# Two row tiles in the last projection of a fused convolution network

## The chip, the core and the metric

The kernel runs on one core of a Trainium2 chip. The metric is device time in microseconds (us) from launch to end, the median of several runs; the profile is one more execution, taken by the hardware profiler. The engines are called as the profile calls them: PE (TensorE, matmuls), PEld (its weight loads), DVE (VectorE), ACT (ScalarE), POOL (GpSimd) and SP (SyncE, which here only issues DMAs). Everything is float32.

## What is computed

The input x holds 8 images of 384 channels by 32 x 32 pixels. Four layers follow each other, each adding to x what it makes of a group normalization of x (32 groups):

```
x = x + conv_attention(gn(x))
x = x + top2_of_4_experts(gn(x))
x = x + depthwise_7x7(gn(x))
x = x + L3(gn(x))
```

The change lies in the last, L3. It makes three branches of the normalized input, mixes them by weights per image and channel, and projects:

```
# branch k of 1, 3, 5: four chunks of 96 channels; chunks 0 and 2 go through
# an MLP (96 -> 12 -> 96, gelu), chunks 1 and 3 through a depthwise k x k conv
a = (x1 + x2 + x3).mean(axis=(2, 3))
g = gelu(a @ fusion_w1 + fusion_b1) @ fusion_w2 + fusion_b2
w = softmax over the 3 branches of g, per image and channel
comb = x1 * w[0] + x2 * w[1] + x3 * w[2]
out = einsum('bchw,cd->bdhw', comb, proj_w) + proj_b
```

## The kernel before

Channels lie on partitions in three tiles of 128 (`NC` = 3), ordered so that the 192 convolved channels come first: all of channel tile 0 (`unit` 0) and the first 64 rows of tile 1. The 64 rows of images q and q + 4 are stacked into one tile of 128 rows, the **pair** q (`unit` 1, four of them; `HB` = 4). An image has `N` = 1024 pixels, worked in two halves of `HF` = 512. The MLPs of all three branches together have 72 hidden rows per image (`MR` = 72); their second matrix is folded with the branch weights and the projection, so that the projection needs only the 72 hidden rows.

**Before the last stage.** The third layer's convolution (`convolve7`, L1065) ends with a group normalization. `fetch3` (L1719 to 1726) loads the four pairs, two DMAs of 64 rows each, eight in all on SP's queue. Four DVE copies (L1849) spread the normalization's scale and shift over the pair's rows (`pair_s`, `pair_t`), ACT applies them (`prepare3`) and DVE transposes the result. The convolutions run as banded matmuls (`convolve3`, L1765 to 1790): unit 1 with 5x5, unit 1 with 3x3, unit 0 with 5x5, unit 0 with 3x3. Between their groups ACT makes banded weights (`wx`, L1539), from `w` which it loads by its own DMA queue, and evicts the sums (`o`, L366). `hidden3` makes the hidden rows and stores them to `hmem`; `reorder` makes copies of the 1x1 branch's input, in the convolutions' row order, in DRAM (`ya0`, `ya1`).

**Branch weights.** During unit 0's 5x5 convolution `branch_mean` and `branch_weights` (L2035 to 2110) run as jobs: PE L2040, a DVE and ACT softmax, and `fac`, the three weights with their scale for each image. POOL's queue then puts `fac` into the convolution's row order by seven DMAs: `fac` to `fmem` in DRAM (L2065, L2067) and from there to `factor` in SBUF (L2072). During the 3x3 convolution of unit 0, `begin` and `complete` (L2120 to 2143) combine the three branches of a unit: a DVE transpose, an ACT scale (L2130), a DVE scalar_tensor_tensor (STT, L2136), then a transpose and an STT more.

**The last stage**, `project3(b)` for b = 0 to 7 (L2180 to L2222). It loads `hid` (72 rows) and `res` (the residual, 3 x 128 rows), completes image b's unit 0 (`c0`), begins that of image b + 1 and, in the first three images, makes the next pair. Six outputs (three channel tiles by two halves) get one PSUM bank each (`po`, six buffers) and three contractions:

- L2197: 72 hidden rows, weights `wm`
- L2200: 128 rows of the pair, with the other image's 64 rows of the weights set to zero
- L2208: 128 rows of `c0`

Between the second and the third PE makes the next image's `wm` in a bank of its own (`pm`, L2149, two buffers), which ACT copies out (L2151). After each L2208 a DVE STT (L2212) adds `po`, the bias `obias` and `res`, and after every second one SP issues the output's DMA (L2219).

The order on PE, DVE, ACT and POOL is the order of the program up to the end of unit 0's 3x3 convolution (`manual_schedule`); in the last stage the build's scheduler sets it, once for all. An engine runs its list in order. A buffer is taken anew when its last reader is done.

Of the kernel before, what the change touches and what calls it, by code (L numbers as in the profile page):

```python
# [18 lines left out]
P = 128  # L19
B, C, H, W = 8, 384, 32, 32  # L20
N = H * W
# [115 lines left out]
def conv_mixer_kernel(ctx: ExitStack, tc: tile.TileContext, a: dict, out: bass.AP):  # L137
# [176 lines left out]
    def affine(o, i, s, t, func=AF.Identity):  # L314
        nc.scalar.activation(o, i, func, bias=t, scale=s)  # L315
# [230 lines left out]
    x2mem = [dram.tile([NC, P, 32 * HP], FP, tag=f"x2_{b}", name=f"x2_{b}") for b in range(B)]  # L546
    y2mem = [dram.tile([NC, P, N], FP, tag=f"y2_{b}", name=f"y2_{b}") for b in range(B)]
    ya0 = [dram.tile([P, N], FP, tag=f"ya0_{b}", name=f"ya0_{b}") for b in range(B)]
    ya1 = [dram.tile([P, N], FP, tag=f"ya1_{q}", name=f"ya1_{q}") for q in range(HB)]
    hmem = [dram.tile([MR, N], FP, tag=f"h{b}", name=f"h{b}") for b in range(B)]  # L550
    fmem = dram.tile([P, 3, B + HB], FP, tag="fac", name="fmem")
    cfmem = dram.tile([2 * B * E * 4, P], FP, tag="cf", name="cfmem")

    def layers(again, early, xst, pre_pool, pp0, pw):
# [1077 lines left out]
        edges = fe.tile([P, 2, B, 5, 4], FP, name="edges")  # L1632
        pair_s, pair_t = (fe.tile([P, HB], FP, name=f"pair_{k}") for k in "st")
        for3 = {}

        def load3():
            for name in "k1 k3 k5 bias3 mw1 mb1 mw2 mw2t fb1 fb2".split():
                for3[name] = load(fe, name)
            for name in ("projb", "proj", "projc"):
                for3[name] = load(fw, name)  # L1640
            gmat["B"] = fe.tile([P, len(blocks), P], FP, name="gmatB")
            nc.sync.dma_start(out=gmat["B"], in_=gmem)

        b7 = load(fe, "b7")
# [74 lines left out]
        def fetch3(q):  # L1719

            y = new_y()
            for half in range(2):
                nc.sync.dma_start(
                    out=y[64 * half : 64 * half + 64, :], in_=y2mem[HB * half + q][1, 0:64, :]
                )
            return y

        def prepare3(unit, q, y=None):

            if unit == 0:  # L1730
                if q == 0:
                    room3(0)
                y = new_xn2().rearrange("p r w -> p (r w)")[:, :N]
                nc.sync.dma_start(out=y, in_=y2mem[q][0])
                affine(y, y, s01[:, 0, q : q + 1], t01[:, 0, q : q + 1])
            else:
                affine(y, y, pair_s[:, q : q + 1], pair_t[:, q : q + 1])
# [10 lines left out]
        def reorder():  # L1748
            def move(o, i):
                nc.gpsimd.dma_start(out=o.rearrange("d r n -> r d n"), in_=i.rearrange("d r n -> r d n"))  # L1750

            for b in range(B):
                ya, y = ya0[b], y2mem[b][0]
                ya = ya.rearrange("(d b a r) n -> b a d r n", a=2, b=2, d=2)
                y = y.rearrange("(a b d r) n -> b a d r n", a=2, b=2, d=2)
                for i, j in product(range(2), repeat=2):
                    move(ya[i, j], y[i, j])
                half, q = b // HB, b % HB
                ya = ya1[q].rearrange("(d b a r) n -> a b d r n", a=2, b=2, d=2)[half]
                y = y2mem[b][1, 0:64, :].rearrange("(b d r) n -> b d r n", b=2, d=2)  # L1760
                for i in range(2):
                    move(ya[i], y[i])
# [41 lines left out]
        with tc.manual_schedule(engines=ORDERED | {mybir.EngineType.Pool}):  # L1804

            for ct in range(NC):
                o = None
                for c in range(8):
# [37 lines left out]
                    if ct == 2 and c == 6:  # L1846
                        for o2, v in ((pair_s, s01), (pair_t, t01)):
                            for half in range(2):
                                nc.vector.tensor_copy(  # L1849
                                    o2[64 * half : 64 * half + 64, :],  # L1850
                                    v[0:64, 1, half * HB : (half + 1) * HB],
                                )
                        for q in range(HB):
                            prepare3(1, q, ys3[q])
# [31 lines left out]
            nc.vector.tensor_copy(s3, s)  # L1886
            nc.vector.tensor_copy(t3, t)
            prepare3(0, 7)
            for _ in range(5):
# [145 lines left out]
            def branch_weights():  # L2035

                pg = banks().tile([P, NC, 3, B])
                for ct in range(NC):
# [19 lines left out]
                for j in range(2):  # L2058
                    nc.vector.tensor_copy(fac[:, j, 1:], wb[:, j, 1:])
                    for o, v in ((fac[:, j, 0], s3), (con[:, j], t3)):  # L2060
# [3 lines left out]
                        )  # L2064
                nc.gpsimd.dma_start(out=fmem[:, :, :B], in_=fac[:, 0])  # L2065
                for half in range(2):
                    nc.gpsimd.dma_start(  # L2067
                        out=fmem[64 * half : 64 * half + 64, :, B:],
                        in_=fac[0:64, 1, :, half * HB : (half + 1) * HB],
                    )  # L2070
                for i in range(4):
                    nc.gpsimd.dma_start(  # L2072
                        out=factor[32 * i : 32 * i + 32],
                        in_=fmem.rearrange("(a b d r) k n -> d b a r (k n)", a=2, b=2, d=2)[
                            i // 2, i % 2
                        ],
                    )

# [61 lines left out]
            def complete(v, unit, q):  # L2140
                c3 = pre.tile([P, N], FP, tag="c3", name="c3")
                nc.vector.transpose(img(c3), os3[unit, 3][:, q])
                add(v, c3, unit, q, 1)

            def weights3(b, pool):

                pm = pool.tile([MR, C], FP, tag="pm", name="pm")
                for j in range(2):
                    nc.tensor.matmul(pm, lhsT=w2[:, j, b], rhs=proj[:, 1 + j], start=j == 0, stop=j == 1)  # L2149
                wm = pre.tile([MR, C], FP, tag="wm", name="wm", bufs=1)  # L2150
                nc.scalar.copy(wm, pm)  # L2151
                return wm

            pairs, c0s, wms = {}, {}, {}

# [4 lines left out]
            def first():  # L2160
                wms[0] = weights3(0, banks(False))
                c0s[0] = begin(0, 0, pre, 2, nc.gpsimd)

# [12 lines left out]
        with tc.tile_pool(name="py", reuse_waits="tile", bufs=2) as py, tc.tile_pool(  # L2176
# [3 lines left out]
            def project3(b):  # L2180
                half, q = b // HB, b % HB
                hid = py.tile([MR, N], FP, tag="hid", name="hid")
                nc.sync.dma_start(out=hid, in_=hmem[b])
                res = py.tile([P, NC, N], FP, tag="res", name="res")
# [4 lines left out]
                if q + 1 < HB and half == 0:  # L2189
                    pair(q + 1, py, HB - 1)  # L2190
                outs = []
                for oc in range(NC):
                    oc_cols = slice(oc * P, (oc + 1) * P)
                    for h in range(2):
                        cols = slice(h * HF, (h + 1) * HF)
                        po = pp.tile([P, HF], FP, tag="pj", name="po")
                        nc.tensor.matmul(  # L2197
                            po, lhsT=wms[b][:, oc_cols], rhs=hid[:, cols], start=True, stop=False
                        )
                        nc.tensor.matmul(  # L2200
                            po, lhsT=projc[:, 1 + half, oc_cols], rhs=pairs[q][:, cols],
                            start=False, stop=False,
                        )
                        outs.append((oc, cols, po))
                if b + 1 < B:
                    wms[b + 1] = weights3(b + 1, pmp)
                for oc, cols, po in outs:
# [3 lines left out]
                    )  # L2211
                    nc.vector.scalar_tensor_tensor(  # L2212
                        out=res[:, oc, cols], in0=po, scalar=obias[:, oc, b : b + 1],
                        in1=res[:, oc, cols], op0=ALU.add, op1=ALU.add,
                    )
                    if cols.start:
# [26 lines left out]
def lay_out(inp):  # L2243
# [78 lines left out]
    for n in KS:  # L2322
        band = np.zeros((2, P, n, W, W), np.float32)
        w = f[f"L3_conv_f{n // 2 + 1}_conv_w"].reshape(192, n, n)
        w = np.concatenate([w, w[P:]]).reshape(2, P, n, n)
# [34 lines left out]

    pc = f["L3_conv_proj_w"][ORDER_B][: 2 * P, ORDER_B].reshape(2, 2, 2, 2, 16, C).swapaxes(1, 3)
    half = np.zeros((2, 2, 2, 2, 16, C), np.float32)
    for h in range(2):
        half[h, :, :, h] = pc[1, :, :, 0]
    o["projc"] = np.concatenate([pc[:1], half]).reshape(3, P, C).swapaxes(0, 1)
    o["projb"] = tiles_b(f["L3_conv_proj_b"])
# [19 lines left out]
```

## Time and profile before

| | us |
|---|---|
| median of 3 runs (3173.9 to 3177.14) | 3174.2 |
| profiled execution | 3172.27 |
| its span, first to last instruction | 3170.5 |
| PE busy | 3023.9 (95% of the span) |
| DVE busy | 1694.7 (53%) |
| ACT busy | 1190.1 (38%) |
| POOL busy | 253.9 (8%) |

In the rows, `L2208 PE MATMUL po<-c,projc 128*128 128x512` means: line 2208, engine PE, a matmul from tiles c and projc into po, with weights of 128 rows by 128 columns and 512 moving columns. A float32 matmul of the program is two PE instructions in the records. `[3.34 <-ACT o L366]` is idle time before the instruction and what ended it. PEclk is the granted TensorE clock as a share of full speed.

The table has the last stage's place in it: PE's first L2197 is at 3030.34 us of the span, its last L2208 ends at 3162.5.

### The profile page before, as it was taken

What the parts mean: (1) busy time and instruction counts of PE and PEld (TensorE: products, weight loads), DVE (VectorE), ACT (ScalarE), POOL (GpSimd) and SP (SyncE); (2) the same over time, 40 slices, a digit from 0 to 9 for tenths busy, and PEclk for the clock granted to TensorE, in tenths of its full rate; (3) what the DMA queues carried; (4) which work ended last, traced back from release to release, by engine and by line L of the source; (5) the groups of instructions that cost most, each with busy time, mean ns of one, the idle gap of its engine ahead of it and who ended that gap; (6) DMA issues with size and microseconds to landing.
All of it is one profiled execution on the core that took longest, in us unless ns stands there. A gap on an engine that the chain in (4) does not pass through costs nothing.

```text
span 3170.5 us, 42235 instructions
## 1 busy us (share of the span) xinstructions
PE 3023.9 (95%) x17740; PEld 1605.6 (51%) x17740; DVE 1694.7 (53%) x2570; ACT 1190.1 (38%) x1356; POOL 253.9 (8%) x415
## 2 busy tenths in 40 slices
PE   4988999999999999999998999999999999886998
PEld 3775434343433334343433576676665666555543
DVE  6998354445444444445445464564554555447164
ACT  3554453535445353535442221212212112446510
POOL 2432000000000000000001100000000000111400
PEclk9999999999999999999999999999999999998999
DMA  6787011011101111011004021121121113867775
GB/s 222 270 280 288 33 41 65 23 62 43 60 25 60 43 43 62 23 62 43 11 25 163 20 64 40 64 64 40 64 64 49 42 44 129 332 223 241 234 226 185
DMA packets 89089, 322.84 MB, mean 102 GB/s; under 512 B 13608, under 2 KB 16000, under 8 KB 84664
## 3 DMA queue, kind: packets, MB, share of 16 engines
q1 hardware_dynamic: 64936, 251.71, 23.5%
q10 hardware_dynamic: 13776, 35.82, 3.6%
q0 software_dynamic: 10176, 32.51, 3.0%
q8 instruction: 141, 2.31, 0.3%
q14 instruction: 60, 0.49, 0.1%
HBM read 211.66 MB, written 111.68 MB: 102 GB/s over the span
## 4 chain that ended last, share of the span: by engine, by line
PE 82%; DVE 8%; DMA 6%; issue 2%; ACT 1%; POOL 1%; SPq 0%; ACTq 0%; POOLq 0%; DVEq 0%
PE ph L1306 16%; PE sc L734 15%; PE av L753 14%; PE p L1217 13%; PE sc L632 7%; PE sc L687 4%; PE sc L809 4%; DMA w<-in_w 3%; DVE stats L213 2%; DVE y L462 2%; PE ps L1783 2%; PE po L2197 1%; PE po L2200 1%; PE po L2208 1%; DVE xt L429 1%
## 5 line engine op out<-in xcount | busy, mean ns | idle before, releaser
L741 ACT ACTIVATE e<-sc 128x1024 f32<-128x1024 f32 x512 | 483.2, 1031 | 608.2 <-PE sc L734 608.1
L1306 PE MATMUL ph<-xn,w 128*128 128x512 f32 x1152 | 504.1, 596 | 3.0 <-ACT xn L315 3.0
L734 PE MATMUL sc<-qT,kT 64*128 64x512 f32 x2048 | 473.9, 602 | 0.0
L753 PE MATMUL av<-e,vT 128*64 128x512 f32 x2048 | 467.8, 599 | 0.0
L1310 ACT ACTIVATE hs<-ph,b 128x512 f32<-128x512 f32 x192 | 131.8, 686 | 705.7 <-PE ph L1306 705.4
L1306 PEld LDWEIGHTS ph<-xn,w 128*128 128x128 f32 x1152 | 218.2, 191 | 264.6 <-issue 258.6
L734 PEld LDWEIGHTS sc<-qT,kT 64*128 64x128 f32 x2048 | 186.9, 186 | 282.0 <-issue 231.1
L753 PEld LDWEIGHTS av<-e,vT 128*64 128x64 f32 x2048 | 135.6, 137 | 316.4 <-issue 316.4
L632 PE MATMUL sc<-y,pw 128*128 128x512 f32 x576 | 249.3, 594 | 0.0
L491 PE MATMUL ps<-xt,wx 64*64 64x256 f32 x3456 | 200.3, 392 | 35.2 <-DVE xt L429 20.1
L1231 DVE TENSOR_TENSOR r<-r,p 128x256 f32<-128x256 f32 x416 | 157.1, 417 | 138.9 <-PE p L1217 138.9
L769 DVE LOAD_MASK_SELECT sm<-av x64 | 0.9, 14 | 417.0 <-PE av L753 417.0
L771 DVE RECIPROCAL inv<-sm 128x512 f32<-128x512 f32 x64 | 214.6, 3353 | 2.2
L491 PEld LDWEIGHTS ps<-xt,wx 64*64 64x64 f32 x3456 | 158.8, 139 | 75.6 <-issue 38.9
L1065 PE MATMUL ps<-xt,wx 64*64 64x256 f32 (+1 forms) x2912 | 159.1, 377 | 22.6 <-ACT wx L1539 11.8
L632 PEld LDWEIGHTS sc<-y,pw 128*128 128x128 f32 x576 | 109.1, 190 | 139.7 <-issue 138.3
L1217 PE MATMUL p<-hs_sum,wsum 128*128 128x256 f32 x768 | 173.6, 379 | 0.0
L1217 PEld LDWEIGHTS p<-hs_sum,wsum 128*128 128x128 f32 x768 | 146.3, 190 | 19.5
L1210 DVE TENSOR_TENSOR hs_sum<-hs,hs_sum 128x768 f32<-128x768 f32 (+1 forms) x192 | 146.9, 779 | 4.9
L1065 PEld LDWEIGHTS ps<-xt,wx 64*64 64x64 f32 x2912 | 109.1, 138 | 70.8 <-ACT wx L1539 14.1
L687 PE MATMUL sc<-pw_v,y 128*128 128x384 f32 x384 | 128.2, 495 | 10.9 <-ACT y L315 10.9
L366 ACT COPY o<-ps 128x2048 f32<-128x2048 f32 x56 | 103.9, 1856 | 81.6 <-PE ps L491 47.4
(320 smaller groups left out, 3246.8 us busy)
## 6 DMA issues: line engine op xcount, KB each, us to landing
raw<-y SPq DMA_DIRECT2D x72, 512.0 KB
y<-raw SPq DMA_DIRECT2D x24, 1536.0 KB
x<-x SPq DMA_DIRECT2D x23, 608.0 KB
xt<-x SPq DMA_DIRECT2D x23, 608.0 KB
w<-in_w ACTq DMA_DIRECT2D x36, 384.0 KB
xn<-in_x SPq DMA_DIRECT2D x24, 512.0 KB
x<-in_x SPq DMA_DIRECT2D x16, 768.0 KB
z<-z POOLq DMA_DIRECT2D x16, 768.0 KB, 4.3
```

The source lines that it names most:

```text
L491: nc.tensor.matmul(ps[64 * d : 64 * d + 64, 2 * i + e, cc], lhsT=w[r, 12 * cc + 6 * e + 3 * d + k, :], rhs=xt0s[ct][r, 16 * d + 4 * u + 2 ...
L632: nc.tensor.matmul(ps[:, h, :], lhsT=w[:, ct, pair, :], rhs=y[:, ct, h * HF : (h + 1) * HF], start=ct == 0, stop=ct == NC - 1,)
L687: nc.tensor.matmul(ps[:, m, :C], lhsT=y[:, ct, (m0 + m) * P : (m0 + m + 1) * P], rhs=pw_v[:, ct, :], start=ct == 0, stop=ct == NC - 1,)
L734: nc.tensor.matmul(sc[:, s, :], lhsT=kTs[b][r, pair, m * P : (m + 1) * P], rhs=qTs[b][r, pair, h * HF : (h + 1) * HF], start=True, stop=True,)
L741: nc.scalar.activation(e, sc, AF.Exp, scale=1.0 if shifted else HD**-0.5)
L753: nc.tensor.matmul(av[64 * s : 64 * s + 64, :], lhsT=vTs[0][:, m, c0 : c0 + 64], rhs=e[:, s, :], start=m == 0, stop=m == N // P - 1,)
L771: nc.vector.reciprocal(inv, sm)
L1065: nc.tensor.matmul(ps[64 * d : 64 * d + 64, 2 * i + e, c % 2, images], lhsT=w[r, d * K7 + k, :], rhs=by_slot(xts[ct])[r, 16 * d + column(c ...
L1210: nc.vector.tensor_add(rows_of(o, hs, s), rows_of(i, hs, s), rows_of(j, hs, s))
L1217: nc.tensor.matmul(ps[:, :QF], lhsT=block(w)[:, e], rhs=rows_of(x, hs, e), start=e == 0, stop=e == E - 1,)
L1231: nc.vector.tensor_tensor(out=o, in0=o, in1=ps[:, :QF], op=op)
L1306: nc.tensor.matmul(ph, lhsT=w1[:, e, ct, dc * P : (dc + 1) * P], rhs=xns[b, h][:, ct, :], start=ct == 0, stop=ct == NC - 1,)
```

## The change

1. **Row tiles.** Of the pair only the image's own 64 rows are contracted, and of the 72 hidden rows 64 lie on the other 64 rows of the array: `hid` and `wm` start at row 64 for images 0 to 3, at row 0 for 4 to 7. The pair's term starts `po`; the hidden term goes to a bank of its own (`ph`, with `pm`'s two buffers). The other 8 hidden rows are loaded and copied twice, to the starts of two 32-row tiles of the pair's half, and are added to `po` by matmuls of 8 rows, on the two tiles in turn.
2. **Sums.** ACT evicts `ph` with the bias into `hp` (three buffers), POOL adds `hp` to `res`, and the DVE STT becomes a `tensor_add` of `po` and `res`.
3. **Loads and copies.** `hid` comes by three DMAs (64, 8 and 8 rows), for image 0 earlier, on POOL's queue; `wm` leaves PSUM by three ACT copies; `c3` has one buffer in place of two.
4. **Unit 1** is interleaved by images in groups of 16 rows: `fetch3` loads a pair by four DMAs of 32 rows, 16 in all; `ya1` and the host's weights follow.
5. **Selection matrices.** `pair_s` and `pair_t` come by four small matmuls with `pick` and one copy; `fac` becomes `factor` by nine matmuls with `perm` and `pick2` and one copy, without the seven DMAs. POOL builds these matrices.

The core of the diff:

```diff
 def fetch3(q):
     y = new_y()
-    for half in range(2):
+    for g in range(4):
         nc.sync.dma_start(
-            out=y[64 * half : 64 * half + 64, :], in_=y2mem[HB * half + q][1, 0:64, :]
+            out=y[32 * g : 32 * g + 32], in_=y2pairs[q][:, 1, 16 * g : 16 * g + 16, :]
         )
...
-                        for o2, v in ((pair_s, s01), (pair_t, t01)):
-                            for half in range(2):
-                                nc.vector.tensor_copy(
-                                    o2[64 * half : 64 * half + 64, :],
-                                    v[0:64, 1, half * HB : (half + 1) * HB],
+                        pp = banks(False).tile([P, 2, HB])
+                        for i, v in enumerate((s01, t01)):
+                            for h in range(2):
+                                nc.tensor.matmul(
+                                    pp[:, i], lhsT=pick[:, h], rhs=v[:64, 1, h * HB : (h + 1) * HB],
+                                    start=h == 0, stop=h == 1,
                                 )
+                        nc.vector.tensor_copy(pair_st, pp)
...
-                nc.gpsimd.dma_start(out=fmem[:, :, :B], in_=fac[:, 0])
-                for half in range(2):
-                    nc.gpsimd.dma_start(
-                        out=fmem[64 * half : 64 * half + 64, :, B:],
-                        in_=fac[0:64, 1, :, half * HB : (half + 1) * HB],
-                    )
-                for i in range(4):
-                    nc.gpsimd.dma_start(
-                        out=factor[32 * i : 32 * i + 32],
...
+                pf = slot.tile([P, 3, B + HB])
+                for i in range(3):
+                    nc.tensor.matmul(pf[:, i, :B], lhsT=perm, rhs=fac[:, 0, i], start=True, stop=True)
+                    for h in range(2):
+                        nc.tensor.matmul(
+                            pf[:, i, B:], lhsT=pick2[:, h], rhs=fac[:64, 1, i, h * HB : (h + 1) * HB],
+                            start=h == 0, stop=h == 1,
+                        )
+                nc.vector.tensor_copy(factor, pf)
...
-                nc.scalar.copy(wm, pm)
+                nc.scalar.copy(wm[at : at + 64], pm[:64])
+                for r in rest:
+                    nc.scalar.copy(wm[r : r + MR - 64], pm[64:])
...
+                own = slice(rest[0], rest[0] + 64)
+                for i in range(n):
+                    oc, cols, _ = outs[i]
+                    term(i, projc[:, 1 + half], pairs[q], own, True)
+                    ph = pmp.tile([P, HF], FP, tag="pm", name="ph")
+                    term(i, wms[b], hids[b], slice(at, at + 64), True, ph)
+                    hp = py.tile([P, HF], FP, tag="hp", name="hp", bufs=3)
+                    affine(hp, ph, 1.0, obias[:, oc, b : b + 1])
+                    nc.gpsimd.tensor_tensor(
+                        out=res[:, oc, cols], in0=res[:, oc, cols], in1=hp, op=ALU.add
+                    )
+                for i in range(n):
+                    r = rest[i % 2]
+                    term(i, wms[b], hids[b], slice(r, r + MR - 64))
...
-                    nc.vector.scalar_tensor_tensor(
-                        out=res[:, oc, cols], in0=po, scalar=obias[:, oc, b : b + 1],
-                        in1=res[:, oc, cols], op0=ALU.add, op1=ALU.add,
-                    )
+                    nc.vector.tensor_add(res[:, oc, cols], po, res[:, oc, cols])
```

`term` is one matmul of the given rows of weights and data; `at` is 64 and `rest` (0, 32) for images 0 to 3, 0 and (64, 96) for 4 to 7; `affine` is an ACT activation (scale and bias).

In the changed program's lists, ACT has in each image the eviction of `ph` 0, then the scale of the next image's `c0`, then evictions 1 to 5, then the three copies of `wm`. PE has the nine selection matmuls ahead of unit 0's 3x3 convolution.

More of the change, by code (lines that the diff above doesn't have):

```diff
@@ L546, in conv_mixer_kernel @@
     x2mem = [dram.tile([NC, P, 32 * HP], FP, tag=f"x2_{b}", name=f"x2_{b}") for b in range(B)]
-    y2mem = [dram.tile([NC, P, N], FP, tag=f"y2_{b}", name=f"y2_{b}") for b in range(B)]
+    y2pairs = [dram.tile([2, NC, P, N], FP, tag=f"y2_{q}", name=f"y2_{q}") for q in range(HB)]
+    y2mem = [y2pairs[b % HB][b // HB] for b in range(B)]
     ya0 = [dram.tile([P, N], FP, tag=f"ya0_{b}", name=f"ya0_{b}") for b in range(B)]
@@ L550, in conv_mixer_kernel @@
     hmem = [dram.tile([MR, N], FP, tag=f"h{b}", name=f"h{b}") for b in range(B)]
-    fmem = dram.tile([P, 3, B + HB], FP, tag="fac", name="fmem")
     cfmem = dram.tile([2 * B * E * 4, P], FP, tag="cf", name="cfmem")
@@ L1632, in layers @@
         edges = fe.tile([P, 2, B, 5, 4], FP, name="edges")
-        pair_s, pair_t = (fe.tile([P, HB], FP, name=f"pair_{k}") for k in "st")
+        pair_st = fe.tile([P, 2, HB], FP, name="pair_st")
+        pick = fe.tile([64, 2, P], FP, name="pick")
         for3 = {}
@@ L1640, in load3, with halves_of_ident, permutations @@
                 for3[name] = load(fw, name)
-            gmat["B"] = fe.tile([P, len(blocks), P], FP, name="gmatB")
+            gmat["B"] = fe.tile([P, len(blocks), P], FP, tag="gmatB", name="gmatB")
             nc.sync.dma_start(out=gmat["B"], in_=gmem)
+            nc.gpsimd.memset(pick, 0.0)
+            for h, b in product(range(2), repeat=2):
+                v = pick[:, h].rearrange("p (a b d r) -> p a b d r", a=2, b=2, d=2)
+                nc.gpsimd.tensor_copy(v[:, :, b, h], halves_of_ident()[:, :, b])
+        def halves_of_ident():
+            return ident[:64, :64].rearrange("p (a b r) -> p a b r", a=2, b=2)
+        def permutations():
+            t = fe.tile([P, len(blocks), P], FP, tag="gmatB", name="perm")
+            perm, pick = t[:, 0], t[:64, 1:3]
+            v = perm.rearrange("p (d b a r) -> p d b a r", d=2, b=2, a=2)
+            i = ident.rearrange("p (a b d r) -> p d b a r", d=2, b=2, a=2)
+            for d, b in product(range(2), repeat=2):
+                nc.gpsimd.tensor_copy(v[:, d, b], i[:, d, b])
+            nc.gpsimd.memset(pick, 0.0)
+            for h, b in product(range(2), repeat=2):
+                v = pick[:, h].rearrange("p (d b a r) -> p d b a r", d=2, b=2, a=2)
+                nc.gpsimd.tensor_copy(v[:, h, b], halves_of_ident()[:, :, b])
+            return perm, pick
         b7 = load(fe, "b7")
@@ L1736, in prepare3 @@
             else:
-                affine(y, y, pair_s[:, q : q + 1], pair_t[:, q : q + 1])
+                affine(y, y, pair_st[:, 0, q : q + 1], pair_st[:, 1, q : q + 1])
             nc.vector.transpose(
@@ L1758, in reorder @@
                 half, q = b // HB, b % HB
-                ya = ya1[q].rearrange("(d b a r) n -> a b d r n", a=2, b=2, d=2)[half]
-                y = y2mem[b][1, 0:64, :].rearrange("(b d r) n -> b d r n", b=2, d=2)
+                ya = ya1[q].rearrange("(d b a r) n -> d b a r n", a=2, b=2, d=2)[half]
+                y = y2mem[b][1, 0:64, :].rearrange("(a b r) n -> b a r n", a=2, b=2)
                 for i in range(2):
@@ L1887, in layers @@
             nc.vector.tensor_copy(t3, t)
+            perm, pick2 = permutations()
             prepare3(0, 7)
@@ L2035, in branch_weights @@
             def branch_weights():
-                pg = banks().tile([P, NC, 3, B])
+                slot = banks()
+                pg = slot.tile([P, NC, 3, B])
                 for ct in range(NC):
@@ L2064, in branch_weights @@
                         )
-                nc.gpsimd.dma_start(out=fmem[:, :, :B], in_=fac[:, 0])
-                for half in range(2):
-                    nc.gpsimd.dma_start(
-                        out=fmem[64 * half : 64 * half + 64, :, B:],
-                        in_=fac[0:64, 1, :, half * HB : (half + 1) * HB],
-                    )
-                for i in range(4):
-                    nc.gpsimd.dma_start(
-                        out=factor[32 * i : 32 * i + 32],
-                        in_=fmem.rearrange("(a b d r) k n -> d b a r (k n)", a=2, b=2, d=2)[
-                            i // 2, i % 2
-                        ],
-                    )
+                pf = slot.tile([P, 3, B + HB])
[7 more added lines that the diff above has]
+                nc.vector.tensor_copy(factor, pf)
                 cb = atile("cb", [NC, B, 3], tag="q")
@@ L2140, in complete, with rows3 @@
             def complete(v, unit, q):
-                c3 = pre.tile([P, N], FP, tag="c3", name="c3")
+                c3 = pre.tile([P, N], FP, tag="c3", name="c3", bufs=1)
                 nc.vector.transpose(img(c3), os3[unit, 3][:, q])
                 add(v, c3, unit, q, 1)
+            def rows3(b):
+                return (64, (0, 32)) if b < HB else (0, (64, 96))
             def weights3(b, pool):
+                at, rest = rows3(b)
                 pm = pool.tile([MR, C], FP, tag="pm", name="pm")
@@ L2149, in weights3, with load_hid @@
                     nc.tensor.matmul(pm, lhsT=w2[:, j, b], rhs=proj[:, 1 + j], start=j == 0, stop=j == 1)
-                wm = pre.tile([MR, C], FP, tag="wm", name="wm", bufs=1)
-                nc.scalar.copy(wm, pm)
-                return wm
-            pairs, c0s, wms = {}, {}, {}
+                wm = pre.tile([P, C], FP, tag="wm", name="wm", bufs=1)
+                nc.scalar.copy(wm[at : at + 64], pm[:64])
+                for r in rest:
+                    nc.scalar.copy(wm[r : r + MR - 64], pm[64:])
+                return wm
+            def load_hid(b, pool, queue, bufs):
+                at, rest = rows3(b)
+                hid = pool.tile([P, N], FP, tag="hid", name="hid", bufs=bufs)
+                queue.dma_start(out=hid[at : at + 64], in_=hmem[b][:64])
+                for r in rest:
+                    queue.dma_start(out=hid[r : r + MR - 64], in_=hmem[b][64:])
+                return hid
+            pairs, c0s, wms, hids = {}, {}, {}, {}
             def pair(q, *args):
@@ L2161, in first @@
                 wms[0] = weights3(0, banks(False))
+                hids[0] = load_hid(0, pre, nc.gpsimd, 1)
                 c0s[0] = begin(0, 0, pre, 2, nc.gpsimd)
@@ L2181, in project3 @@
                 half, q = b // HB, b % HB
-                hid = py.tile([MR, N], FP, tag="hid", name="hid")
-                nc.sync.dma_start(out=hid, in_=hmem[b])
+                if b > 0:
+                    hids[b] = load_hid(b, py, nc.sync, 2)
                 res = py.tile([P, NC, N], FP, tag="res", name="res")
@@ L2190, in project3, with term @@
                     pair(q + 1, py, HB - 1)
[L2191 to L2204, printed above, removed]
+                at, rest = rows3(b)
+                outs = [
+                    (oc, slice(h * HF, (h + 1) * HF), pp.tile([P, HF], FP, tag="pj", name="po"))
+                    for oc in range(NC) for h in range(2)
+                ]
+                n = len(outs)
+                def term(i, w, x, rows, start=False, ps=None):
+                    oc, cols, po = outs[i]
+                    nc.tensor.matmul(
+                        po if ps is None else ps, lhsT=w[rows, oc * P : (oc + 1) * P],
+                        rhs=x[rows, cols], start=start, stop=ps is not None,
+                    )
[9 more added lines that the diff above has]
+                        out=res[:, oc, cols], in0=res[:, oc, cols], in1=hp, op=ALU.add
+                    )
+                for i in range(n):
+                    r = rest[i % 2]
+                    term(i, wms[b], hids[b], slice(r, r + MR - 64))
                 if b + 1 < B:
@@ L2211, in project3 @@
                     )
-                    nc.vector.scalar_tensor_tensor(
-                        out=res[:, oc, cols], in0=po, scalar=obias[:, oc, b : b + 1],
-                        in1=res[:, oc, cols], op0=ALU.add, op1=ALU.add,
-                    )
+                    nc.vector.tensor_add(res[:, oc, cols], po, res[:, oc, cols])
                     if cols.start:
@@ L2324, in lay_out @@
         w = f[f"L3_conv_f{n // 2 + 1}_conv_w"].reshape(192, n, n)
-        w = np.concatenate([w, w[P:]]).reshape(2, P, n, n)
+        w = np.stack([w[:P], np.repeat(w[P:].reshape(4, 1, 16, n, n), 2, 1).reshape(P, n, n)])
         for x in range(W):
@@ L2359, in lay_out @@
     o["proj"] = tiles_b(f["L3_conv_proj_w"][:, ORDER_B])
-    pc = f["L3_conv_proj_w"][ORDER_B][: 2 * P, ORDER_B].reshape(2, 2, 2, 2, 16, C).swapaxes(1, 3)
-    half = np.zeros((2, 2, 2, 2, 16, C), np.float32)
+    pc = f["L3_conv_proj_w"][ORDER_B][:, ORDER_B]
+    half = np.zeros((2, 2, 64, C), np.float32)
     for h in range(2):
-        half[h, :, :, h] = pc[1, :, :, 0]
-    o["projc"] = np.concatenate([pc[:1], half]).reshape(3, P, C).swapaxes(0, 1)
+        half[h, h] = pc[P : P + 64].reshape(2, 2, 16, C).swapaxes(0, 1).reshape(64, C)
+    pc = pc[:P].reshape(1, 2, 2, 2, 16, C).swapaxes(1, 3)
+    o["projc"] = np.concatenate([pc.reshape(1, P, C), half.reshape(2, P, C)]).swapaxes(0, 1)
     o["projb"] = tiles_b(f["L3_conv_proj_b"])
```

## The prediction

> **What bounds the kernel now.** I read the busy shares first, then the last stage cut into stretches of 20 us, then the chain that ended last, then the timelines around the two earlier places that the change touches. The columns of the stretches: busy time of PE, PEld, DVE, ACT and POOL with the number of instructions, the granted clock, the DMA share, GB/s.
>
> ```profile
> 3030.00:3050.00 20.00, 19.66 (x42) 8.67 (x43) 15.37 (x16) 1.52 (x2) 0.00 (x0) 0.91 0.70 238
> 3050.00:3070.00 20.00, 20.00 (x48) 8.79 (x47) 17.03 (x18) 2.77 (x3) 0.00 (x0) 1.00 0.87 268
> 3090.00:3110.00 20.00, 20.00 (x50) 8.89 (x49) 10.22 (x11) 2.10 (x3) 0.00 (x0) 1.00 0.66 219
> ```
>
> PE has no gap from 3050 on, ACT and POOL are nearly idle, and DVE is nearly full only while pairs are made. The chain agrees (start, duration, what):
>
> ```profile
> 3089.43 0.86 PE po L2200 x2
> 3090.29 1.29 PE pm L2149 x4
> 3091.58 5.15 PE po L2208 x12
> 3096.73 0.86 PE po L2197 x2
> ```
>
> A PE instruction with 512 columns costs 5.15/12 = 0.429 us, whatever its rows. An image has 36 of them and one pm: 36 x 0.429 + 1.29 = 16.74 us, and indeed 3096.73 - 3079.97 = 16.76. Images 1 and 7 have no pm between (15.46). So fewer slots on PE are time, if nothing else becomes late.
>
> **The gain on PE.** Two matmuls on different 64-row tiles do run at once here: the attention's scores have the same form, 64 rows by 128 columns by 512.
>
> ```profile
> 1201.97 3.70 PE L734 MATMUL sc<-qT,kT 64*128 64x512 f32 x16
> ```
>
> 16 instructions in 3.70 us are 0.23 each: two a slot. So pair and hidden rows, 24 instructions, take 12 slots, 5.15 us. The 12 instructions of 8 rows have no row in this trace. If two 32-row tiles work at once, as the 64-row tiles do, they take 6 slots, 2.57; if one waits for the other, 12 slots, 5.15. I take 2.57, the nearest row being L734. Each change of form opens a gap: where PE passes from L753 to L734 I read starts 522 ns apart in place of 429, and a little more in the slot behind. Three changes an image at 0.15 give 0.45. Nominally: 5.15 + 2.57 + 1.29 + 5.15 + 0.45 = 14.6, a gain of 2.1 an image. [...]
>
> **The wait that takes the place of it.** `ph` has two banks, so `ph` 3 may start only when ACT has evicted `ph` 1. In ACT's list the scale of the next image's `c0` stands between evictions 0 and 1, and it waits for DVE's transpose, which stands behind the last add of the image before. Prices:
>
> ```profile
> L1310 ACT ACTIVATE hs<-ph,b 128x512 f32<-128x512 f32 x192 | 131.8, 686 | 705.7 <-PE ph L1306 705.4
> ...
> L2130 ACT ACTIVATE c<-c,factor 128x1024 f32<-128x1024 f32 x7 | 8.0, 1148 | 41.0 <-DVE c L2129 41.0
> L2129 DVE STREAM_TRANSPOSE c<-o 128x1024 f32<-128x1024 f32 x6 | 7.4, 1234 | 0.0
> ```
>
> Counted from an image's start: last add done at 0.9 (0.75, row L2212, behind 0.15 of handing over), transpose 2.1, scale 3.35, eviction 1 at 4.05. `ph` 3 would have begun at 3 x 0.86 + 0.15 = 2.7: PE stands for 1.35. Evictions 2 to 5 then keep pace (0.69 against 0.86). Period: 14.6 + 1.35 = 16.0, a gain of 0.76 of the 2.1. Queued behind the scale on ACT are five evictions and the three copies of `wm` (0.47 by row L2151 and two smaller ones, 0.3 each by my estimate from the 686 and 474 ns of larger tiles); these end well ahead of the next image.
>
> Image 1 is worse: DVE has the STT of the pair's making (1.28) between adds 4 and 5, so the stall is 2.6, and its pm lies between now: 17.1 against 15.46, +1.6. Images 2 to 6: 5 x -0.76 = -3.8. Image 7 has neither scale nor pm: 13.45 against 15.46, -2.0.
>
> POOL's sums: 1264 ns each (row L1196, same shape), six an image, 7.6 us of 16: they fit. `tensor_add` in place of the STT on DVE: same shape, 0. The hidden DMAs of 8 rows: DMA share is 0.66 to 0.87; `res` of image b + 2 lands about 5 us ahead of need by my count, so 0, at worst 1 us an image.
>
> **Image 0.** What is late first is the branch weights:
>
> ```profile
> 2989.40 2.18 PE L2040 MATMUL ps<-g,x 96*128 96x8 f32 x18
> ...
> 2994.92 12.17 PE L1783 MATMUL ps<-xt,wx 64*64 64x256 f32 x192 [3.34 <-ACT o L366]
> ...
> 2997.78 0.22 DVE L2061 SCALAR_TENSOR_TENSOR xt<-wb,k,s 128x8 f32<-128x8 f32 x1
> ```
>
> The nine selection matmuls stand ahead of the convolution that starts at 2994.92, and need `fac`, done at 2998.0. They are 18 instructions, as L2040 is: 2.18 us. PE goes on at 3000.1 instead, +5.15; behind them wait all of the convolution, ACT's evictions of it and so `c0`. Some 0.6 comes back, since the first scale (idle 0.62 at 3006.98) waits for no factor DMA: +4.5 by the convolution's end. The stage itself starts sooner after it, because `hid` 0 was loaded early (PE idled 2.62 for it). But `res` 0, on SP's queue behind a `ya` load that waits for DVE, is issued at about 3031 instead of 3025.95 and lands some 8.3 later (3025.95 to 3034.5 before), 3039.3. Eviction 3 needs the third `hp` back, thus POOL's first add, thus `res` 0: 3039.3 + 1.26 + 0.69, and the handings over, put `ph` 5 at 3041.8. Then 8-row terms, pm and c0: 9.0 + 0.45, and a half slot: 3051.7, and 0.5 for a clock halved by the pause (the clock is 0.91 in the first stretch, with such a pause of 2.62). Before: 3047.7. So +4.5, the branch weights included.
>
> **Ahead of it, the pairs.**
>
> ```profile
> 2828.86 6.92 SPq L1723 DMA_DIRECT2D y<-y  x8
> ...
> 2838.22 1.23 ACT L1539 ACTIVATE wx<-w,parity 128x448 f32<-128x448 f32 x2 [9.18 <-DMA y<-y]
> 2839.35 1.84 ACT L366 COPY o<-ps 128x2048 f32<-128x2048 f32 x1
> 2841.24 4.72 PE L1065 MATMUL ps<-xt,wx 64*64 64x256 f32 x56 [9.50 <-ACT o L366]
> ```
>
> ACT's load of `w` waits 9.2 us for a completion counter that it shares with one of the eight pair loads (the second), and PE waits for ACT. Those loads move at about 230 KB/us. With 16 loads of 128 KB the counter's earlier user is the tenth instead of the second: 1280 KB in place of 512, +768/230 = +3.3, which I take as 3.4, if 32 partitions move as fast as 64. The trace has no such load; at half the rate it is +9, at best 0. [...] I find no slack behind it: DVE, POOL's 2.9 us for `gn_s` and ACT follow in a row up to PE at 2860.41.
>
> `pair_st` by matmuls: eight small instructions, 1.0 by row L240, on a PE that then waits 4.09 for DVE anyway: 0. Built matrices: ten-odd POOL copies of 0.3 (POOL is busy 8%): 0, at worst 1.
>
> **Sum**: +3.4 + 4.5 + 1.6 - 3.8 - 2.0 = +3.7 on the profiled execution: 3172.27 + 3.7 = 3176.0. The median lies 1.9 above that execution: **3178**. About 0.2% (6.3 us) is what a measurement of this kernel can tell from no change; +3.7 is within it.
>
> **Rivals.**
>
> 1. *The 8-row tiles work one after the other.* Twelve slots in place of six, 8 x 2.57 = +20.6: 3198. For it: both tiles serve the same accumulation pattern with 8 rows only, and nothing in the trace shows 32-row tiles. Against: L734. It decides from the first image: a 5.15 in place of a 2.57 there. This is the rival on the slower side. Chance 0.13.
> 2. *Loads and sums are later than I count*: pair loads at half rate (+5.6 more), `res` or POOL's sums late by 1 us an image (+8), the clock halved by each stall. Any one or two: 3184 to 3196. For it: DMA share 0.87 and DVE 17 of 20 at 3050 to 3070. Chance 0.22.
> 3. *The stall is not there, or the early delays are absorbed.* If ACT's scale comes without waiting, six images gain 1.35 more, -8.1: 3170; and if the pair loads cost nothing, 3166. With the branch weights absorbed too (-4.5), 3162. For it: between 2870 and 2990 the chain often waits for DMAs (w, 11.7% of it), in which a delay could vanish. Chance 0.20.
>
> The forecast itself, 3171 to 3184, has 0.45. In it "within 0.2%" holds about 0.32 and "slower" 0.12. All cases: faster 0.20, same 0.35, slower 0.45. Range: 3163 (rival 3 nearly whole) to 3198 (rival 1).
>
> **What would show it.** PE's idle before the convolution of L1065 near 2841 at 12.9 in place of 9.5; PE's idle before unit 0's 3x3 convolution at 3000, released by DVE; 8-row matmuls in pairs a few ns apart; a PE wait of 1.3 us on ACT once an image; images of 16.0 us and a last one of 13.5. It is wrong if the 8-row matmuls stand 429 ns apart, if POOL's adds take over 1.3 us, or if PE waits for `po` or DMA.

## The result, and the profile after

The changed kernel takes 3218.3 us (median of four, 3211.4 to 3227.8) against 3175.5 before on the same chip: ratio 1.014, interval 1.011 to 1.016. It is some 43 us slower, far above the range. A second measurement on another occasion (below, with the experiments) gave 1.0151 (1.0135 to 1.0168).

Where the time went is read best as the delay of the profiled execution after against the one before, at points that both have. A row is the growth of the delay since the row above. Image ends are the starts of the image's last add (L2212 before, L2263 after).

| from the point above to | before | after | delay grows by | forecast |
|---|---|---|---|---|
| first matmul of `convolve7` | 2669.1 | 2673.7 | +4.6 | 0 |
| first convolution of the pairs | 2860.4 | 2887.5 | +22.4 | +3.4 |
| matmuls of the branch weights end | 2991.6 | 3017.0 | -1.6 | 0 |
| unit 0's 3x3 convolution starts | 2994.9 | 3027.7 | +7.3 | +5.15 |
| it ends | 3025.0 | 3060.1 | +2.3 | -0.6 |
| image 0 ends | 3048.2 | 3089.7 | +6.4 | about 0 |
| image 1 ends | 3063.5 | 3109.2 | +4.3 | +1.6 |
| images 2 to 6 end | 3147.0 | 3202.0 | +9.2 | -3.8 |
| image 7 ends | 3162.5 | 3217.7 | +0.2 | -2.0 |

The sum is 55.2, the difference of the spans. That is more than the 43 of the medians: the profiled execution (3227.8) is the slowest of its four. The 4.6 of the first row lie ahead of all changed work and are no part of the change: the other profile of the same kernel reaches that point at 2667.0.

The first large loss, in the timeline and in stretches (columns as in the prediction):

```profile
2833.99 28.84 SPq L1744 DMA_DIRECT2D y<-y  x16
2863.97 1.23 ACT L1539 ACTIVATE wx<-w,parity 128x448 f32<-128x448 f32 x2 [29.45 <-DMA y<-y]
2867.00 6.20 PE L1065 MATMUL ps<-xt,wx 64*64 64x256 f32 x56 [29.78 <-ACT o L366]
```

```profile
2840.00:2848.00 8.00, 0.00 (x0) 0.00 (x0) 0.00 (x0) 0.00 (x0) 0.00 (x0) 0.50 0.13 53
2848.00:2856.00 8.00, 0.00 (x0) 0.00 (x0) 0.00 (x0) 0.00 (x0) 0.00 (x0) 0.50 0.13 52
```

No engine computes for almost 26 us (2838.1 to 2864.0), and the DMA share is 0.13, as much as two of 16 DMA engines. Before, the eight loads of 64 rows kept all of them busy:

```profile
2833.00:2837.00 4.00, 0.00 (x0) 0.00 (x0) 0.00 (x0) 0.00 (x0) 0.00 (x0) 0.62 1.03 229
```

The branch weights, after. PE waits for the softmax, does its nine matmuls, and goes on with the convolution at 3027.69:

```profile
3018.52 1.86 ACT L366 COPY o<-ps 128x2048 f32<-128x2048 f32 x1 [0.41 <-ACT wx L1539]
...
3023.31 0.57 PE L2092 MATMUL ps<-xt,perm 128*128 128x8 f32 x2 [6.27 <-DVE xt L2086]
3023.81 1.01 PE L2094 MATMUL ps<-xt,perm 64*128 64x4 f32 x4
...
3027.69 13.54 PE L1804 MATMUL ps<-xt,wx 64*64 64x256 f32 x192
```

And one image of the last stage (image 4, on PE from 3146.5 to 3164.4), cut by what PE does: pairs, the rest of the pairs, 8-row matmuls, pm and the first of c0, c0 without its last 1.4 us:

```profile
3146.50:3150.30 3.80, 3.71 (x15) 1.68 (x14) 2.42 (x4) 2.42 (x4) 1.27 (x1) 1.00 0.88 272
3150.30:3153.30 3.00, 2.96 (x10) 0.98 (x10) 2.93 (x3) 1.85 (x3) 2.94 (x2) 1.00 0.45 126
3153.30:3156.10 2.80, 2.80 (x13) 1.06 (x12) 1.22 (x1) 0.77 (x2) 2.80 (x3) 1.00 1.01 407
3156.10:3159.70 3.60, 3.60 (x8) 1.61 (x7) 0.00 (x0) 0.82 (x2) 1.93 (x2) 0.53 0.84 269
3159.70:3163.00 3.30, 3.30 (x8) 1.42 (x8) 2.20 (x4) 0.59 (x2) 0.00 (x0) 1.00 0.10 31
```

PE has next to no idle time, as the forecast wanted it, but the granted clock is halved just behind the 8-row matmuls, for 3.4 us (3156.3 to 3159.7) or, in every other image, for 6.8. The 8-row matmuls themselves do run two at a time:

```profile
3153.35 2.84 PE L2237 MATMUL po<-hid,wm 8*128 8x512 f32 x12
3156.13 2.69 PE L2175 MATMUL pm<-proj,w 128*72 128x384 f32 x4
```

12 in 2.84 us are six slots; the pm behind them, at half the clock, takes twice its 1.29.

### The profile page after: what moved, and what is told of

It is laid out like the page before. It is cut to its first block, busy times and chain, and to the rows that moved or that the text cites. A ratio compares the mean times of both kernels' runs of the same rounds, so it can differ in the third digit from the quotient of the medians.

```text
span 3225.7 us, 42745 instructions
## 1 busy us (share of the span) xinstructions
PE 3046.8 (94%) x17862; PEld 1610.5 (50%) x17862; DVE 1701.0 (53%) x2568; ACT 1228.5 (38%) x1420; POOL 325.5 (10%) x473
## 5 line engine op out<-in xcount | busy, mean ns | idle before, releaser
L1539 ACT ACTIVATE wx<-w,parity 128x320 f32<-128x320 f32 (+2 forms) x152 | 83.8, 603 | 148.5 <-DMA y<-y 29.4
```

## The experiments

Each kernel is the changed one with the edit shown. Ratios are to the kernel before, in the same job. Two profiled executions of the changed kernel serve for comparison; its own ratio lies at 1.014 to 1.015.

**1. Pair loads of 16 rows.** [Source and target of each DMA begin with 16.]

```diff
-                nc.sync.dma_start(
-                    out=y[32 * g : 32 * g + 32], in_=y2pairs[q][:, 1, 16 * g : 16 * g + 16, :]
-                )
+                for h in range(2):
+                    (nc.sync, nc.gpsimd)[h].dma_start(
+                        out=y[32 * g + 16 * h : 32 * g + 16 * h + 16],
+                        in_=y2pairs[q][h, 1, 16 * g : 16 * g + 16, :],
+                    )
```

> The changed kernel, with each of the 16 pair loads split into two of 16 rows, so that the slowest dimension of a load is 16 and not 2 (half of the 32 loads issued by SP, half by POOL). Theory A: a load whose source begins with a dimension of 2 is carried by two of the 16 DMA engines (DMA share 0.13 and 53 GB/s while ACT and PE wait). Then the wait of ACT near 2864, 29.4 us, falls to about 10, the DMA share in it rises over 0.5, and the median falls by 17 to 22 us. Rival B: tiles of 32 or 16 partitions load slowly whatever the split; then the share stays near 0.13 and the time does not fall.

Measured: 3196.2 us, ratio 1.0085 (1.0065 to 1.0106), by the ratios 16 to 21 us below the changed kernel. From the first matmul of `convolve7` to the first convolution of the pairs it takes 193.9 us; the changed kernel 213.8, the one before 191.3.

```profile
2828.00:2832.00 4.00, 0.07 (x1) 0.00 (x0) 0.70 (x4) 0.00 (x0) 0.99 (x3) 0.73 1.05 260
2832.00:2836.00 4.00, 0.00 (x0) 0.00 (x0) 0.00 (x0) 0.00 (x0) 3.44 (x8) 0.50 0.94 226
```

```profile
2824.20 11.27 SPq L1745 DMA_DIRECT2D y<-y  x16
...
2836.50 1.23 ACT L1539 ACTIVATE wx<-w,parity 128x448 f32<-128x448 f32 x2 [11.12 <-DMA y<-y]
```

Share 0.13 became 1.0, ACT's wait 29.4 became 11.1. Theory A holds; rival B, slow tiles, falls. The edit also gave half of the loads to POOL's queue, but that is not what did it: from 2829 to 2835, with pair loads alone, the packets of SP's queue took 51% of the 16 engines (POOL's 48%); without this edit they took 13% (2840 to 2862). Three forms of the load are measured: 64 rows on both sides, share 1.03 (229 GB/s, the kernel before); a source of 2 x 16 x 1024, share 0.13, which is 2 of 16 (53 GB/s, the changed kernel); 16 rows on both sides, 0.94 to 1.05 (226 to 260 GB/s, this run).

**2. 40 and 32 hidden rows.**

```diff
-                nc.scalar.copy(wm[at : at + 64], pm[:64])
+                nc.scalar.copy(wm[at : at + 32], pm[32:64])
+                nc.scalar.copy(wm[at + 32 : at + 40], pm[64:])
                 for r in rest:
-                    nc.scalar.copy(wm[r : r + MR - 64], pm[64:])
+                    nc.scalar.copy(wm[r : r + 32], pm[:32])
...
-                    term(i, wms[b], hids[b], slice(r, r + MR - 64))
+                    term(i, wms[b], hids[b], slice(r, r + 32))
```

> The changed kernel, with the 72 hidden rows divided as 40 on the 64-row tile and 32 on the 32-row tiles, in place of 64 and 8: as many matmuls of the same 512 columns, one ACT copy more an image. Theory A: the clock is halved because a stretch of 2.8 us of matmuls with only 8 rows counts as little activity; with 32 rows it stays at 1.0, images 2 to 6 take 16.0 to 16.4 us in place of 17.9 and 19.5, and the median falls by 12 to 18 us. Rival B: the clock is halved by PE's waits for ACT (0.7 us in each image); then nothing changes but 1 us.

Measured: 3207.8 us, 1.0117 (1.0100 to 1.0134), by the ratios 6 to 11 us less; in the profile images 2 to 6 take 17.6, then 16.2 four times. The stage's other end, image 7, takes 14.0. The same stretch of the span in both kernels, first the changed one, then this:

```profile
3140.00:3160.00 20.00, 19.87 (x55) 7.95 (x54) 9.99 (x10) 7.57 (x13) 8.93 (x6) 0.85 0.61 201
```

```profile
3140.00:3160.00 20.00, 19.87 (x68) 7.85 (x66) 12.32 (x12) 8.38 (x14) 12.75 (x9) 1.00 0.76 242
```

PE is busy for the same 19.87 us, with 68 matmuls in place of 55, at a clock of 1.00 in place of 0.85. PE's stop for ACT is still there. Theory A holds, at less in the median than expected. The 17.6 of image 2 holds a halved window too, behind another cause: from 3101.19 to 3104.60 PE works 1.92 of 3.41 us, and the next window is at 0.50.

**3. Branch weights by DMA.** The nine matmuls and the copy are replaced by the DMAs of the kernel before, with the rows of `fmem` in the new order.

```diff
-                pf = slot.tile([P, 3, B + HB])
-                for i in range(3):
-                    nc.tensor.matmul(pf[:, i, :B], lhsT=perm, rhs=fac[:, 0, i], start=True, stop=True)
...
+                nc.gpsimd.dma_start(out=fmem[:, :, :B], in_=fac[:, 0])
+                for half in range(2):
+                    nc.gpsimd.dma_start(
+                        out=fmem.rearrange("(c d r) k n -> d c r k n", c=4, d=2)[half, :, :, :, B:],
+                        in_=fac[0:64, 1, :, half * HB : (half + 1) * HB],
+                    )
...
```

> The changed kernel, with the branch weights brought into the convolution's order by seven DMAs through DRAM again, in place of nine matmuls and a copy. Theory A: PE's wait for the softmax ahead of unit 0's last convolution (6.3 us), the 4.4 us of the matmuls and the halved clock behind them cost 9.5 us in all; of these 8 to 9.5 come back. Rival B: only the 5 us that PE stands later come back, the clock being low anyway at this place.

Measured: 3218.9 us, 1.0142 (1.0125 to 1.0159): no gain that the median shows. In the profile the place itself gains 7.6: from the end of the branch weights' matmuls to the stage's first matmul 35.2 us, against 42.9 and 42.6 in the two profiles of the changed kernel (the stage's first matmul is the first into `ph`). The convolution starts 3.2 us behind the matmuls, not 10.7:

```profile
3019.48 13.31 PE L1805 MATMUL ps<-xt,wx 64*64 64x256 f32 x192 [3.17 <-ACT o L366]
```

The profile comes close to A's lower end. That the median does not follow is left open: 7.6 us are 0.24%, no more than the intervals of this ratio and of the changed kernel's leave room for, and the stretch from the first matmul of `convolve7` to the branch weights, which waits for DMAs, takes 342 to 350 us in profiles of kernels that do not differ there (347.4 in this one).

**4. The scale on DVE.** `begin` takes a flag, and in the last stage c0's scale is `nc.vector.tensor_scalar`.

```diff
-                    c0s[b + 1] = begin(0, b + 1)
+                    c0s[b + 1] = begin(0, b + 1, dve=True)
```

> The changed kernel, with the scale of the next image's c0 done by DVE in the last stage, so that ACT evicts ph without the scale between. Theory A (8-row matmuls halve the clock): PE's stop of 0.7 to 1.35 us in the middle of the pairs goes, the clock is still halved once an image or in two of three, and the median falls by 4 to 9 us. Rival B (the stop halves the clock): the clock stays at 1.0 from image 2 on and the median falls by 18 us or more. Third way: DVE becomes the bound in the images with pairs, and nothing is gained there.

Measured: 3207.7 us, 1.0109 (1.0092 to 1.0126), by the ratios 9 to 13 us less, at the upper end of A's range or beyond it. Images 3 to 5 take 16.9, with one halved window each:

```profile
3120.00:3140.00 20.00, 20.00 (x66) 8.84 (x65) 14.66 (x13) 7.16 (x12) 13.04 (x9) 0.91 0.73 234
```

PE has no gap any more (20.00), and the clock is 0.91. So it is not PE's stop that halves the clock in these images: rival B of both runs falls. With the stop, every other image has a second halved window.

Image 6 of this run takes 15.2, and its clock is not halved, though its 8-row matmuls stand in a row like the others'. It shows how near the limit is. The clock windows that follow the one with most of the 8-row matmuls, of image 5 and of image 6:

```profile
3159.98:3163.39 3.41, 3.41 (x6) 1.50 (x5) 0.69 (x1) 1.41 (x3) 2.07 (x2) 0.50 0.64 207
3177.05:3180.46 3.41, 3.41 (x9) 1.52 (x8) 1.85 (x3) 1.41 (x3) 1.93 (x2) 1.00 0.58 239
```

The windows before them start at 3156.57 and 3173.63. In image 5 the 8-row matmuls run from 3156.09 to 3158.87, in image 6 from 3173.03 to 3175.80; pm and c0 follow. So 2.30 us of 8-row matmuls in a window cost the clock of the next, and 2.17 us did not: where the window falls on the work decides.

**5. Six `hp` buffers.** One number, 3 to 6.

> The changed kernel with six hp buffers in place of three. Theory A: in image 0 PE stands 5 us behind an eviction that waits for POOL's first add to give a buffer back, and that add waits for the residual of image 0; with six buffers the evictions run ahead of POOL, that stop goes, and images 0 and 1 end 4 to 9 us earlier. Rival B: the residual's arrival sets the end of image 0 in any case (the last add needs it), so that DVE is late instead and less than 2 us come back.

Measured: 3219.9 us, 1.0143 (1.0128 to 1.0158), not to be told from the changed kernel. In the profile image 0 takes 26.3 us from the stage's first matmul in place of 29.7; image 1 takes 19.55 as before. PE's stop is 2.45 in place of 4.99, and another release stands behind it: ACT's list has scales that wait for DVE. Between A and B.

**6. The 8-row matmuls between the pairs.**

```diff
-                for i in range(n):
-                    r = rest[i % 2]
-                    term(i, wms[b], hids[b], slice(r, r + MR - 64))
+                    if i % 2:
+                        for j in (i - 1, i):
+                            r = rest[j % 2]
+                            term(j, wms[b], hids[b], slice(r, r + MR - 64))
```

> The changed kernel with the 8-row matmuls set between the pairs, two outputs' worth after each two outputs, in place of all six behind the pairs: same work, two more changes of form a image pass (about 0.15 us each, twice). Theory A: it is the share of a clock window (3.4 us) filled by 8-row matmuls that halves the clock; spread, they fill a half or less, the clock stays at 1.0 in most images, and these take 15.5 to 16.5 us in place of 17.9 and 19.5: 10 to 17 us in all. Rival B: any such stretch is enough, or the changes of form cost more than 0.3 us each; then nothing is gained or it is slower.

Measured: 3204.0 us, 1.0103 (1.0087 to 1.0118), by the ratios 15 us below the changed kernel of the same job. Images 2 to 6 take 15.5, all at full clock; image 7 takes 14.3:

```profile
3120.00:3140.00 20.00, 20.00 (x66) 7.65 (x66) 13.64 (x17) 6.47 (x10) 8.94 (x6) 1.00 0.86 271
```

The same 8-row work, only spread, does not halve the clock from image 1 on. And the stop for ACT's scale is gone too, since the 8-row matmuls fill that time. The seven changes of form of such an image cost (15.52 - 14.16)/7 = 0.19 us each, where 14.16 is 18 slots of 0.429, pm and c0.

**7. All of it together** (1, 2, 3, 4 and 5).

> All of it together: pair loads of 16 rows on two queues, 40 + 32 hidden rows, the branch weights by DMA, the scale by DVE, six hp buffers. Theory A, by the terms measured one at a time: 20 for the loads, 14 for the clock, 8 for the branch weights, 5 for the stop in the pairs, 4 to 9 for image 0: 3218 less 51 to 56, thus 3162 to 3167, 0.2 to 0.3% below the kernel before, with images of 14.8 us from the fourth on. Rival B: DVE, which then has 17 us of work in the images with pairs, or the DMA share becomes the bound in the stage, and it ends level with the kernel before or up to 10 us above.

Measured: 3168.4 us, 0.9985 (0.9974 to 0.9996). Images 3 to 6 take 15.2 to 15.5, not 14.8. Image 0 takes 26.7 from the stage's first matmul, image 1 17.5, and from the first matmul of `convolve7` to the first convolution of the pairs it takes 197.8, not the 193.9 of run 1: what is missing lies in these places.

**8. The changed kernel again.** 

> The changed kernel once more, beside the others on the same chip: to tell what of its 43 us repeats. If the order of the first 260 us and the place of the clock windows vary from execution to execution, the median lies within 8 us of 3218 and the stage's images again take 17.9 and 19.5 us by turns.

Measured: 3224.1 us, 1.0151 (1.0135 to 1.0168), with images of 19.55 and 17.90 by turns. The pattern repeats to 0.01 us; the start (first matmul of `convolve7` at 2667.0 in place of 2673.7) does not.

**9 to 11. Better versions.** Run 9 is run 7 with 64 and 8 rows, the 8-row matmuls spread as in 6, and the scale of the pairs made in the stage on DVE too. Run 10 is run 9 with 40 and 32 rows. Run 11 is run 9 with all scales on ACT.

> The combined kernel with 64 + 8 rows again, the 8-row matmuls spread between the pairs, and all scales of the last stage on DVE, those of the pairs too, so that ACT only evicts. Theory A: image 0 took 26.7 us in the combined kernel because ACT's evictions stood behind two scales that waited for DVE (PE stopped 2.4 us), and the clock was halved for three windows behind it; without the scales that stop goes, the halved windows go or fall to one, image 0 takes 19 to 22 us, image 1 15 to 16, the others 15.0 to 15.5: 6 to 10 us less than the combined kernel, 3158 to 3163. Rival B: DVE gets 1.3 us more an image and two more in image 0, and holds up c0 or the adds: no gain over the combined kernel (3168).

Measured: 3166.5 us, 0.9982 (0.9973 to 0.9990): the lowest ratio of all, 0.18% below the kernel before, but not to be told from run 7 (0.9974 to 0.9996), and so by the time nearer to B than to A. Image 0 takes 23.3, with one halved window, image 1 16.9. What ends image 0 late now is DVE: two of its STTs take 2.28 and 2.23 us in place of 1.28 while POOL adds, and stand ahead of its adds, which PE waits for.

```profile
3036.57 10.84 POOL L2259 TENSOR_TENSOR res<-res,hp 128x512 f32<-128x512 f32 x6 [26.65 <-DMA res<-y]
...
3040.58 2.28 DVE L2166 SCALAR_TENSOR_TENSOR c<-c,factor,c 128x1024 f32<-128x1024 f32 x1
...
3044.06 2.23 DVE L2166 SCALAR_TENSOR_TENSOR c<-ya,factor,c 128x1024 f32<-128x1024 f32 x1
3046.21 2.47 DVE L2273 TENSOR_TENSOR res<-po,res 128x512 f32<-128x512 f32 x4
3046.94 1.06 PE L2246 MATMUL po<-c,projc 64*128 64x512 f32 x1 [2.23 <-DVE res L2273]
```

> The kernel of the run before, with 40 + 32 rows. Theory A (the clock follows how much of the array a window keeps busy): spread already keeps the clock up in the steady images, so that it adds nothing there, but in image 0, where a halved clock lasts as long as the matmuls are thin, 32 rows bring it back sooner: 0 to 3 us less. Rival B: the longer ACT list (four copies) and the larger loads make it 1 to 3 us slower.

Measured: 3173.6 us, 1.0004 (0.9995 to 1.0013); a miss for A. The clock was halved in image 0 for five windows, though PE had no gap in them (four are shown):

```profile
3034.40:3037.80 3.40, 3.40 (x10) 0.94 (x9) 3.40 (x4) 0.00 (x0) 0.00 (x0) 0.50 1.01 394
3037.80:3041.20 3.40, 3.40 (x10) 0.75 (x6) 3.40 (x5) 1.37 (x2) 1.21 (x1) 0.50 1.04 300
3041.20:3044.60 3.40, 3.40 (x10) 1.19 (x8) 3.40 (x4) 0.69 (x1) 3.40 (x3) 0.50 1.02 407
3044.60:3048.00 3.40, 3.40 (x8) 0.83 (x7) 3.37 (x3) 0.69 (x1) 3.40 (x3) 0.50 0.84 223
```

It came back behind pm and the first of c0 (0.50 up to 3051.5, 1.00 behind it). In image 1 the same pairs run at the full clock (0.59 us a matmul from 3056.5 on, 1.06 in image 0), but in image 0 they did not bring the halved one back.

> The kernel of the first run of these three, with the scales back on ACT. Theory A: in the steady images the 8-row matmuls between the pairs give ACT the time that the scale takes, so these stay at 15.5; images 0 and 1 keep the stop and the halved windows, and end 5 to 8 us later than with DVE's scales. Rival B: the place of the scales does not matter, since DVE's transposes and sums set the pace of images 0 to 2: within 3 us of it.

Measured: 3171.1 us, 0.9998 (0.9988 to 1.0008), 4.5 us above run 9. Images 2 to 6 stay at 15.5; image 1 takes 20.4, with three halved windows. Theory A, except in image 0, which is no later than in run 9 (22.8 from the stage's first matmul, against 23.3).

## Why the prediction was wrong, point by point

- **The pair loads: the step that failed first.** "+768/230 = +3.3, which I take as 3.4, if 32 partitions move as fast as 64". The condition looked at the partitions of the target, and it did not hold: with 32 rows in the target and a first dimension of 2 in the source the share was 0.13, with 16 rows on both sides 0.94 to 1.05 (run 1). The term is some 20 (22.4 in the table; run 1 takes 19.9 of it away). I gave the upper end as 9, "at half the rate"; two engines of 16 are an eighth of them, and about a quarter of the rate in the rows (53 against 229 GB/s). The counter that ACT shares with a load, and the lack of slack behind it, were right: the tenth load ends after 1280 KB, which at 53 KB a us is 24 us, and ACT went on there. In the traces the second load before and the tenth after signal the semaphore of ACT's `w` load; they land at 2837.68 and 2863.44, and ACT issues at 2837.70 and 2863.46.
- **Images 2 to 6: "5 x -0.76 = -3.8"** came out at +9.2. This is the second step that failed. The slots are as forecast: 8-row matmuls two at a time, 0.19 for a change of form (0.15 said), a stop for ACT's scale. With the clock kept up (run 2) the period is 16.21, forecast 16.0. What is missing from the sum is the clock behind the thin matmuls, 1.7 or 3.4 us an image. I named a halved clock only for pauses, and looked for PE's idle time; the clock fell with PE busy. Images 1 and 7 fail by the same term: 7 takes 14.0 in run 2, and 15.7 here.
- **The branch weights**: +5.15 forecast, +7.3 measured: the nine matmuls go in groups of 1.5 us, 4.4 in all, not in 2.2, at a clock of 0.50 (from 3019.8 on, in the middle of PE's wait of 6.27). In place of the 0.6 that I gave back the convolution took 2.3 more, with more of it at the halved clock (12.6 us at 0.50, 6.3 before), but this is not shown to be the change's: runs 1, 2, 4 and 6, with the same matmuls ahead of it, take 29.3 to 30.5 for the convolution, and run 3, without them, 32.0.
- **Image 0**: the chain res 0, POOL's first add, third `hp`, eviction, `ph` is as described (PE stood 4.99 us for it). The cost was too small by 6: the halved clock lasted four windows, not half a us, and POOL's adds took 1.7 us each in the mean, not 1.26, beside DVE's STTs.
- **Right**: no loss from `pair_st` (PE waits 2.67 us for DVE there, 4.09 before); the loads of res in time in the steady images.
- **Small slips in the sums**, which change nothing: image 1 at 14.6 and 2.6 makes 17.2, not 17.1; image 7 at 14.6 less pm makes 13.3, not 13.45; `res` 0 took 8.55 by the figures given, not 8.3.
- **Rivals**: 1 (tiles one after the other) did not happen. 2 had the loads at half rate and clocks halved by stalls; its direction is right, both sizes are too small. 3 fell: nothing was absorbed, and ACT's stop was there.

What stays open: why run 3 gains 7.6 us in the profile and nothing clear in the median; and by what measure the clock's windows count a matmul's rows. The runs bracket the limit: with pm and c0 in the rest of the window, 2.17 us of 8-row matmuls keep the clock and 2.30 lose it (run 4); with 64-row pairs in the rest, about 1.5 us keep it (run 6) and 1.95 lose it (image 1 of the changed kernel). With 32 rows in place of 8, 2.7 us of them keep it (run 2).

## What to carry to other kernels

Look at the DMA share of a load whose form is new, whatever its bytes: a nice interleaved layout with a leading 2 in the source kept 0.13 of the 16 DMA engines busy here, and the same bytes with 16 first on both sides 0.94 to 1.05 (run 1). Matmuls with few rows were not free here even where the slots were counted right: in a row they cost 1.7 or 3.4 us an image by the clock, and spread between the 64-row ones the clock stayed at 1.00 from image 1 on (run 6). So look at the granted clock in stretches as short as its windows (3.4 us here). A small step moved onto PE makes PE wait for all that the step waits for (6.27 us here).

## What the runs showed of the hardware

- The clock changed in steps of 3.4 us (the halved stretches in the last stage last 3.4, 6.8, 10.2, 13.7 or 17.1 us). In images 1 to 7 of the changed kernel it fell to 0.50 behind a window of 3.41 us with 1.95 to 2.78 us of 8-row matmuls, with PE busy all the time; with 32 rows in place of 8 (run 2), or the 8-row matmuls spread (run 6), it stayed at 1.00 in such images. In image 0 of run 10 a halved clock stayed for 17 us, up to 3047.3 under pairs of 64 and 40 rows and the 32-row matmuls between them; in image 1 such pairs run at the full clock (0.59 us a matmul, 1.06 in image 0).
- In the changed kernel's last stage DVE's STT of `c` (both inputs in SBUF) took 2.12 to 2.40 us in place of 1.28 when it started in the middle of a POOL add or less than 0.1 us ahead of one. When it started 0.2 us or more ahead of the add it took 1.28 to 1.33, and the add got longer (up to 2.25 us; 1.53 in the mean of all, 1.26 clear of the STTs). DVE's adds of a PSUM and an SBUF tile did not get longer in image 0 of run 9 (0.68 in the mean of six), where the first of them start beside POOL's adds.
